# Sequence 1's loads and broadcasts in another order, its layer norm statistics on ScalarE, two scalings on GpSimd

## The chip, the cores and the metric

The kernel runs on one core of a Trainium2 chip. The metric is the device time of one execution in microseconds (us). The engines are called PE (TensorE), DVE (VectorE), ACT (ScalarE), POOL (GpSimd) and SP (SyncE, which here only issues DMA transfers).

## What is computed

A residual x of 2 sequences by 512 tokens by 512 channels goes through four layers, each between two layer norms: `x = x + layernorm(layer(layernorm(x)))`. The layers are a Mamba block, a gated feed-forward layer with 4-bit weights, a small attention inside each token, and a feed-forward layer with an expert. The change lies in the first layer norm and in the Mamba block:

```python
def _layernorm(x, axis=-1, eps=1e-05):
    m = jnp.mean(x, axis=axis, keepdims=True)
    v = jnp.var(x, axis=axis, keepdims=True)
    return (x - m) / jnp.sqrt(v + eps)

def _L0_attn_ref(hidden_states, W_in, conv_w, conv_b, W_x, W_dt, b_dt, A_log, D, W_out):
    D_IN, N, K, R = 1024, 16, 4, 32
    proj = hidden_states @ W_in.T
    x, gate = (proj[..., :D_IN], proj[..., D_IN:])
    xpad = jnp.pad(x, ((0, 0), (K - 1, 0), (0, 0)))
    xc = conv_b
    for j in range(K):
        xc = xc + conv_w[:, j] * xpad[:, j:j + L, :]
    x = silu(xc)
    ssm = x @ W_x.T
    ts, Bm, Cm = (ssm[..., :R], ssm[..., R:R + N], ssm[..., R + N:])
    ts, Bm, Cm = rms_forward(ts), rms_forward(Bm), rms_forward(Cm)
    dt = softplus(ts @ W_dt.T + b_dt)
    A = -jnp.exp(A_log)
    def step(state, inp):
        dt_t, B_t, C_t, u_t = inp
        dA = jnp.exp(dt_t[..., None] * A)
        state = state * dA + (dt_t * u_t)[..., None] * B_t[:, None, :]
        y = jnp.einsum('bdn,bn->bd', state, C_t)
        return (state, y)
    ...
    y = ys + x * D
    y = y * silu(gate)
    return y @ W_out.T
```

`rms_forward` divides by the root of the mean square over the last axis.

## The kernel before

The residual lies in SBUF as eight tiles of 128 tokens by 512 channels, four for each sequence: x0 to x3 for sequence 0, x4 to x7 for sequence 1. Inside the Mamba block the work is turned: 128 channels lie on the partitions and the 512 tokens of a sequence along the free axis, so the 1024 inner channels make eight groups c.

**The head** runs from the start to about 65 us. It normalises sequence 0, projects it into the eight groups (weights `w_x0_*`), convolves, multiplies by W_x into the "ranks" (the 32 rows of dt and the 16 of B and of C) and normalises those in `ranks_norm(0)`. The gate weights `w_g0_0` to `w_g0_2` (L111, in `w4`) are loaded on SP, and the first gate group and half of the second, `half_gate` (L652), are multiplied. `ranks_rows` transposes the normalised ranks (L536); `ranks_out` (L539) copies the dt rows with ScalarE (L541) and the B and C rows, "bc", with VectorE (L542), and writes bc to a DRAM tile, scr. From there `states` (L547) reads it back 16 times on SP (L554), each time two states' rows broadcast over all 128 partitions, 512 KB: the tiles B_0 to B_7 and C_0 to C_7. Behind the last of these broadcasts on SP stand the four x tiles of sequence 1 (`load_x`, L83), and behind those the packed words of the second layer's weights.

**The scan** is a list of 16 items k, one for each pair of sequence and channel group, each in eight steps of two states: 128 steps s. The loop over s writes an order out by hand:

```python
order = [(b, c) for b in range(B) for c in range(NCH)]
```

For each step ScalarE takes two exponentials of 128x511 into one of two PSUM buffers, da (L1039); VectorE multiplies du by the B tile into bx (L1055) and runs the recurrence over 128x1024 in one instruction (TENSOR_TENSOR_SCAN, L1059); GpSimd multiplies bx by the C tile (L1065); and PE adds the two halves into the output, py, with an identity as weights (L1087). The exponentials of step s+2 go into the buffer that scan s has read. There are six bx buffers. For each item ScalarE copies dt into PSUM (L1047) and VectorE multiplies it by u (du, L1053); `fin` multiplies the finished item into its gate (L1093), and dt of the next item comes from a small matmul (L562) and ScalarE's softplus (L567), which changes the activation table. "bx_k_g" below is step g of item k of sequence 0.

**Beside the scan** PE works through one long list, the generator `stream()`: the gates of sequence 0 (L741), the transposes of the normalised sequence 1 (L821), its projections, its ranks (`ranks1`) and their transposed rows (`rows1`), the gates of sequence 1, the output projection, and the second layer for sequence 0. What follows a matmul on the other engines is a small job, spawned with a lag counted in half steps of the scan. A gate's job is three rows of ScalarE (th, g, th: L714, L715, L716) and a product on GpSimd (L719). `norm_job` is such a job: it takes the statistics of x4 to x7 with VectorE's BATCH_NORM instructions, L798 and L799, then ve (L125, variance plus epsilon) on VectorE and, on GpSimd, the power -1/2 (L127) and the product of mean and that, times -1 (L136, L137). `ranks_norm` is run for sequence 1 as a job too; of it the two scalings of the mean squares are L513 and L514 ("rr"), on VectorE. `words_job` unpacks the 4-bit weights between the scan's steps.

Before the scan's loop a call of `pin()` makes each engine keep the order in which the program was written, so an instruction waits for all that stand ahead of it on its engine. SP's transfers are spread over eight completion lanes in turn; from the ninth broadcast on, each issue follows the landing of an earlier one.

Of the kernel before, what the change touches and what calls it, by code (L numbers as in the profile page):

```python
# [9 lines left out]
F32 = mybir.dt.float32  # L10
# [3 lines left out]
ALU = mybir.AluOpType  # L14
# [42 lines left out]
def tile_sandwich(  # L57
# [48 lines left out]
    wgt = const.tile([P, KH, NE], F32, name="wgt")  # L106


    def w4(src, name, chunks=KH, cols=PW):
        t_ = wst.tile([P, KH, PW], F32, tag="w4", name=name)  # L110
        nc.sync.dma_start(out=t_[:, :chunks, :cols], in_=src)  # L111
        return t_

    def moments(srcs, name):
# [311 lines left out]
    with ExitStack() as mamba:  # L426
# [21 lines left out]
        def mbank(name):  # L448
            return ps_m.tile([P, S], F32, tag="m", name=name)
# [18 lines left out]
        def w_in(part, b, c):  # L468

            key = "w", part, b, c // 2  # L470
            if key not in st:
                st[key] = w4(W_in[part * NCH // 2 + c // 2], f"w_{'xg'[part]}{b}_{c // 2}")
            return st[key]
# [28 lines left out]
        def ranks_norm(b, ps):  # L502
# [7 lines left out]
            )  # L510
            nc.vector.tensor_reduce(ss[:, :, 1:], sq[:, :, R_DT // N_ST :], AX.X, ALU.add)
            r = stat.tile([P, TB, 3], F32, tag="rr", name=f"rr{b}")
            nc.vector.tensor_scalar(r[:, :, 0], ss[:, :, 0], 1.0 / R_DT, 1e-6, ALU.mult, ALU.add)  # L513
            nc.vector.tensor_scalar(r[:, :, 1:], ss[:, :, 1:], 1.0 / N_ST, 1e-6, ALU.mult, ALU.add)  # L514
            yield 1
            if b:
                nc.gpsimd.tensor_tensor(r, r, mhalf3, ALU.pow)
# [21 lines left out]
        def ranks_out(b, pt):  # L539
            bc = st["bc"] = jrow(f"bc{b}")  # L540
            nc.scalar.copy(dtT[b][:R_DT, :], pt[:R_DT])  # L541
            nc.vector.tensor_copy(bc[R_B:N_ROW], pt[R_B:N_ROW])  # L542
            sc = dram.tile([N_ROW - R_B, S], F32, tag=f"scr{b}", name=f"scr{b}")
            nc.sync.dma_start(out=sc, in_=bc[R_B:N_ROW])
            scr.append(sc)
# [27 lines left out]
        with ExitStack() as p1:  # L573
# [73 lines left out]
            root = stat.tile([P, 1], F32, tag="root", name="root", bufs=1)  # L647
            nc.scalar.activation(root, half[:, 0:1], AF.Sqrt)

            half_gate = mbank("pg0_1")  # L650
            for k in range(KH // 2):
                nc.tensor.matmul(  # L652
                    half_gate, w_in(1, 0, 0)[:, k, P : 2 * P], xT[0][:, k, :], start=(k == 0), stop=False
                )
            for _ in ranks_norm(0, pr):
                pass
            ranks_out(0, ranks_rows(0, bank1(0, "pt0")))

            for gi in range(NGI):
                if gi + 1 < NGI:  # L660
                    states(0, gi + 1, "B")
                states(0, gi, "C")
            last = states(0, 0, "B")
            gw.word()
            dt_out(0, 0, dt_in(0, 0, bank1(0, "pv0_0")))
            with tc.issue_after(last.ins):
                load_x(1)
            pin()

        g1p = pool(mamba, "mg1", 1)  # L670
# [4 lines left out]
        with ExitStack() as p2:  # L675
# [75 lines left out]
            def gate(b, c):  # L751
                w = w_in(1, b, c)
                if c + 2 - c % 2 < NCH:
                    w_in(1, b, c + 2 - c % 2)
                if (b, c) == (0, 1):
                    turns.append([f"pg{b}_{c}", None])
                    ps = half_gate
                    yield from in_proj(b, ps, w, c % 2, KH // 2)
                else:
                    ps = yield from bank(f"pg{b}_{c}")  # L760
                    yield from in_proj(b, ps, w, c % 2)
                spawn(gate_job(b, c, ps), 2)
# [30 lines left out]
            def norm_job(b, name):  # L793

                mv = stat.tile([P, TB, 2], F32, tag="mv", name=f"mv_{name}")
                for i, src in enumerate(xs(b)):
                    s6 = stat.tile([P, 6], F32, tag="st", name=f"st_{name}_{i}")
                    nc.vector.bn_stats(s6, src)  # L798
                    nc.vector.bn_aggr(mv[:, i, :], s6)  # L799
                    yield 1  # L800
                yield 1
                rs = rstd(mv, name)
                nm = minus_mean(mv, rs, name, TB, True)
                yield 3
                for i in range(TB):
                    yield 2
# [293 lines left out]

            pe = stream()
            spawn(words_job(), 4)
            spawn(norm_job(1, "n1"), 12)

            d0 = jrow("d0")
            nc.vector.tensor_mul(d0, u[0][0], st["dt", 0, 0])
# [373 lines left out]
```

## Time and profile before

| what | us |
|---|---|
| time, median of 3 runs | 957.5 (957.22 to 958.73) |
| the profiled execution's own time | 955.66 |
| its span (first to last instruction) | 953.7 |
| busy: PE | 860.8 |
| busy: VectorE | 672.4 |
| busy: GpSimd | 486.8 |
| busy: ScalarE | 424.1 |
| TensorE clock granted, mean share of full | 0.965 |
| the 128 scans of VectorE (L1059), busy | 291.4 |
| the 127 products with B (L1055), busy | 152.8 |

"Busy" sums the time in which an engine executes; waiting is not in it. The scan stage runs from about 65 to 600 us; behind it come the rest of the second layer and the third and fourth layers, in which PE does most of the work. In rows of the profile `out<-in` names the program's buffers, and the part in square brackets says how long the engine stood before the instruction and what released it. In the chain of waits each row gives start, duration and what the program's end was traced back through.

### The profile page before, as it was taken

To read this page: it belongs to the slowest core of one execution; us is meant where nothing else is said; L and a number is where in the kernel's file an instruction comes from. 1 tells how busy PE (TensorE), PEld (TensorE's weight loads), DVE (VectorE), ACT (ScalarE), POOL (GpSimd) and SP (SyncE) were. 2 spreads that over 40 slices of the span, in tenths; PEclk is the share of its full clock that TensorE was granted. 3 is DMA by queue.
4 is the path that set the end of the run, shared out by engine and by line. 5 is a ranking of instruction groups with operands and counts; after the bars stand their busy time and mean duration, and the time that the engine had idled before them with its cause. 6 is when DMAs were issued, how large, how long until landed. Compare 5 with 4: busy or idle time off the path is not lost.

```text
span 953.7 us, 7163 instructions
## 1 busy us (share of the span) xinstructions
PE 860.8 (90%) x2188; PEld 385.4 (40%) x2188; DVE 672.4 (71%) x780; ACT 424.1 (44%) x638; POOL 486.8 (51%) x356
## 2 busy tenths in 40 slices
PE   6989778789999889589999999999999998999994
PEld 3433333334533434134434444444544444455441
DVE  5877999999999998999999995535600024525225
ACT  4356675656666655476655640125320013412122
POOL 7746796677877787876877884440000000011002
PEclk9989999888999999889999999999999999999998
DMA  6449111010002854200111103445222231100101
GB/s 201 156 141 376 52 37 38 30 37 30 22 23 91 293 194 142 89 0 0 45 44 45 30 9 125 153 156 198 57 65 74 60 101 44 67 12 23 56 0 44
DMA packets 43816, 80.08 MB, mean 84 GB/s; under 512 B 7774, under 2 KB 20937, under 8 KB 43778
## 3 DMA queue, kind: packets, MB, share of 16 engines
q1 hardware_dynamic: 41506, 73.64, 23.4%
q0 software_dynamic: 1984, 5.47, 1.6%
q10 hardware_dynamic: 288, 0.52, 0.1%
q8 instruction: 17, 0.28, 0.1%
q14 instruction: 21, 0.17, 0.1%
HBM read 68.37 MB, written 11.24 MB: 83 GB/s over the span
## 4 chain that ended last, share of the span: by engine, by line
PE 48%; DVE 24%; issue 9%; POOL 7%; DMA 3%; ACT 2%; SPq 0%; DVEq 0%; POOLq 0%; ACTq 0%
DVE bx L1059 10%; DVE bx L1055 6%; PE py L1087 6%; PE pd L1408 6%; POOL bx L1065 5%; PE pup L1345 5%; PE fo L1198 4%; PE fg L371 4%; PE fu L371 4%; PE fo L1261 3%; PE fu L984 3%; PE fg L984 3%; PE po L1176 3%; PE po L953 2%; DVE u L483 2%
## 5 line engine op out<-in xcount | busy, mean ns | idle before, releaser
L1065 POOL TENSOR_TENSOR bx<-bx,C 128x1024 f32<-128x1024 f32 x128 | 301.8, 2358 | 117.4 <-DVE bx L1059 94.2
L1059 DVE TENSOR_TENSOR_SCAN bx<-da,bx 128x1024 f32<-128x1024 f32 x128 | 291.4, 2277 | 0.1
L1087 PE MATMUL py<-bx,ident 128*128 128x512 f32 x480 | 234.9, 620 | 41.4 <-POOL bx L1065 36.3
L1039 ACT ACTIVATE da<-dt,A 128x511 f32<-128x511 f32 x256 | 176.6, 691 | 170.1 <-DVE bx L1059 163.4
L1087 PEld LDWEIGHTS py<-bx,ident 128*128 128x128 f32 x480 | 90.8, 197 | 168.1 <-issue 91.7
L1055 DVE TENSOR_TENSOR bx<-du,B 128x1024 f32<-128x1024 f32 x127 | 152.8, 1203 | 5.7 <-DMA B<-scr 2.2
L1274 DVE TENSOR_TENSOR it<-it,fu 128x512 f32<-128x512 f32 (+1 forms) x11 | 7.5, 686 | 75.2 <-PE fu L371 75.2
L385 POOL TENSOR_TENSOR sd<-ve,half 128x4 f16<-128x4 f16 x2 | 2.1, 1042 | 110.7 <-DVE ve L383 110.7
L1345 PE MATMUL pup<-hT_l,wup 128*128 128x512 f32 x128 | 57.8, 606 | 0.0
L741 PE MATMUL pg<-xT,w_g 128*128 128x512 f32 x116 | 56.5, 619 | 0.0
L1408 PE MATMUL pd<-wdn,hid 128*128 128x512 f32 x128 | 55.3, 593 | 0.0
L127 POOL TENSOR_TENSOR rs_lo<-ve_lo,mhalf 128x1 f32<-128x1 f32 x8 | 5.4, 680 | 76.7 <-DVE ve_lo L125 76.7
L371 PE MATMUL fg<-hT_f,wg 128*128 128x512 f32 (+1 forms) x88 | 41.9, 614 | 0.7 <-ACT hT_f L171 0.7
L984 PE MATMUL fg<-hT_f,wg 128*128 128x512 f32 (+1 forms) x88 | 42.1, 597 | 0.0
L984 PE MATMUL fu<-hT_f,wu 128*128 128x512 f32 (+1 forms) x88 | 40.7, 592 | 0.0
L483 DVE SCALAR_TENSOR_TENSOR u<-px,ch,u 128x511 f32<-128x511 f32 (+2 forms) x48 | 35.8, 746 | 6.9 <-ACT u L476 5.8
L1261 PE MATMUL fo<-wd,it 128*128 128x512 f32 (+1 forms) x88 | 40.5, 603 | 0.0
L371 PE MATMUL fu<-hT_f,wu 128*128 128x512 f32 (+1 forms) x88 | 39.8, 593 | 0.0
L1198 PE MATMUL fo<-wd,it 128*128 128x512 f32 (+1 forms) x88 | 38.0, 594 | 1.8 <-DMA wd<-wd_d 1.8
L1408 PEld LDWEIGHTS pd<-wdn,hid 128*128 128x128 f32 x128 | 24.2, 190 | 30.7 <-issue 30.1
L1345 PEld LDWEIGHTS pup<-hT_l,wup 128*128 128x128 f32 x128 | 24.3, 193 | 28.8 <-issue 28.8
L1273 ACT ACTIVATE it<-fg 128x512 f32<-128x512 f32 (+1 forms) x11 | 6.6, 597 | 65.7 <-PE fg L371 65.7
(238 smaller groups left out, 1164.8 us busy)
## 6 DMA issues: line engine op xcount, KB each, us to landing
wo<-in_W_outT SPq DMA_DIRECT2D x20, 512.0 KB
B<-scr SPq DMA_DIRECT2D x16, 512.0 KB
C<-scr SPq DMA_DIRECT2D x16, 512.0 KB
wg<-wgu_d SPq DMA_DIRECT2D x10, 512.0 KB
wu<-wgu_d SPq DMA_DIRECT2D x10, 512.0 KB
w_x<-in_W_in SPq DMA_DIRECT2D x8, 512.0 KB
wgu_d<-w_gu POOLq DMA_DIRECT2D x16, 256.0 KB, 2.4
w_g<-in_W_in SPq DMA_DIRECT2D x8, 512.0 KB
```

The costliest lines, as they stand in the source:

```text
L371: nc.tensor.matmul(ps[:m], w[:, kc, e * P : e * P + m], hT[:, kc, :], start=(kc == 0), stop=(kc == KH - 1),)
L741: nc.tensor.matmul(ps, w[:, k, ts(e, P)], xT[b][:, k, :], start=(k == 0), stop=(k == KH - 1))
L984: nc.tensor.matmul(ps[:m], wt[j][a][:, kc, e * P : e * P + m], hT[:, kc, :], start=(kc == 0), stop=(kc == KH - 1),)
L1039: nc.scalar.activation(das[s % 2][:, i, 1:], st["dt", b, c][:, 1:], AF.Exp, scale=A[:, c, n : n + 1])
L1055: nc.vector.tensor_mul(bx, st["du"].unsqueeze(1).to_broadcast([P, NG, S]), Bbs[b][gi])
L1059: nc.vector.tensor_tensor_scan(flat, das[s % 2].rearrange("p n t -> p (n t)"), flat, 0.0, ALU.mult, ALU.add)
L1065: nc.gpsimd.tensor_mul(bxs[s], bxs[s], Cbs[b][s % NGI])
L1087: nc.tensor.matmul(st["y"], ident, bx[:, i, :], start=False, stop=last)
L1198: nc.tensor.matmul(fo[t], its[i][:m, ts(t, P)], w[:m, e], start=(i == 0), stop=(i == len(IC) - 1),)
L1261: nc.tensor.matmul(fo[t], its[i][:m, ts(t, P)], w[:m], start=(i == 0), stop=(i == len(IC) - 1),)
L1345: nc.tensor.matmul(ps, w[:, kc, ts(e, P)], src[kc], start=(kc == 0), stop=(kc == KH - 1))
L1408: nc.tensor.matmul(pd, hid[kc][:, ts(i, P)], wdn[kc], start=(kc == 0), stop=(kc == INT // P - 1),)
```

## The change

- **Loads and broadcasts.** `w4` keeps the instructions that it issues in a list. The x tiles of sequence 1 no longer follow the last broadcast; they go on SP right behind the newest gate weights issued at that point, `w_g0_0`, ahead of `w_g0_1`, `w_g0_2` and the write of scr. The broadcasts of sequence 0 were issued as B1 C0 B2 C1 B3 C2 B4 C3 B5 C4 B6 C5 B7 C6 C7 B0; they are issued as B1 B2 C0 B3 C1 B4 C2 B5 C3 B6 C4 B7 C5 C6 C7 B0.
- **The gate in the head.** Three of the four matmuls of the second gate are done in the head, ahead of `ranks_norm(0)`, and one is left for the stream, where it was two and two.
- **Ranks of sequence 1.** The two scalings of the mean squares go from VectorE to GpSimd, and the bc copy from VectorE to ScalarE, behind the dt copy.
- **Statistics of sequence 1.** In `norm_job` the BATCH_NORM instructions are replaced by two passes of ScalarE for each tile: Identity with scale -1/512 and a running sum into `mv`, which gives minus the mean; then Square with that as bias and a running sum, which gives 512 times the variance. Their full outputs go to a scratch tile. ve (now with the scale 1/512), the power and the product are GpSimd's; the factor -1 goes. The job starts with a lag of 2 instead of 12.

The order written for each engine changes with it. On ScalarE the passes stand between exponentials: after those of step 1 and of step 2 the two of x4, after steps 3 and 4 those of x5, around step 6 those of x6, around step 8 those of x7. The applications of the norm (L150) and the transposes of the four tiles come about one step later, as do the convolutions of the channel groups 3 to 6 of sequence 1; the first nibble of one of the unpacked words comes a step earlier. Counted in rows of the instruction order, in which a run of equal instructions is one row, VectorE goes from 763 to 751, ScalarE from 508 to 517, PE from 626 to 628, GpSimd from 360 to 362, and SP stays at 214; the number of activation table loads in the order is 39 in both.

```diff
--- before.py
+++ after.py
@@ -106,9 +106,11 @@
     wgt = const.tile([P, KH, NE], F32, name="wgt")
 
 
+    issued = []
+
     def w4(src, name, chunks=KH, cols=PW):
         t_ = wst.tile([P, KH, PW], F32, tag="w4", name=name)
-        nc.sync.dma_start(out=t_[:, :chunks, :cols], in_=src)
+        issued.append(nc.sync.dma_start(out=t_[:, :chunks, :cols], in_=src))
         return t_
 
     def moments(srcs, name):
@@ -510,8 +512,9 @@
             )
             nc.vector.tensor_reduce(ss[:, :, 1:], sq[:, :, R_DT // N_ST :], AX.X, ALU.add)
             r = stat.tile([P, TB, 3], F32, tag="rr", name=f"rr{b}")
-            nc.vector.tensor_scalar(r[:, :, 0], ss[:, :, 0], 1.0 / R_DT, 1e-6, ALU.mult, ALU.add)
-            nc.vector.tensor_scalar(r[:, :, 1:], ss[:, :, 1:], 1.0 / N_ST, 1e-6, ALU.mult, ALU.add)
+            eng = nc.gpsimd if b else nc.vector
+            eng.tensor_scalar(r[:, :, 0], ss[:, :, 0], 1.0 / R_DT, 1e-6, ALU.mult, ALU.add)
+            eng.tensor_scalar(r[:, :, 1:], ss[:, :, 1:], 1.0 / N_ST, 1e-6, ALU.mult, ALU.add)
             yield 1
             if b:
                 nc.gpsimd.tensor_tensor(r, r, mhalf3, ALU.pow)
@@ -539,7 +542,10 @@
         def ranks_out(b, pt):
             bc = st["bc"] = jrow(f"bc{b}")
             nc.scalar.copy(dtT[b][:R_DT, :], pt[:R_DT])
-            nc.vector.tensor_copy(bc[R_B:N_ROW], pt[R_B:N_ROW])
+            if b:
+                nc.scalar.copy(bc[R_B:N_ROW], pt[R_B:N_ROW])
+            else:
+                nc.vector.tensor_copy(bc[R_B:N_ROW], pt[R_B:N_ROW])
             sc = dram.tile([N_ROW - R_B, S], F32, tag=f"scr{b}", name=f"scr{b}")
             nc.sync.dma_start(out=sc, in_=bc[R_B:N_ROW])
             scr.append(sc)
@@ -647,11 +653,13 @@
             root = stat.tile([P, 1], F32, tag="root", name="root", bufs=1)
             nc.scalar.activation(root, half[:, 0:1], AF.Sqrt)
 
-            half_gate = mbank("pg0_1")
-            for k in range(KH // 2):
+            first_gate = mbank("pg0_1")
+            for k in range(KH - 1):
                 nc.tensor.matmul(
-                    half_gate, w_in(1, 0, 0)[:, k, P : 2 * P], xT[0][:, k, :], start=(k == 0), stop=False
+                    first_gate, w_in(1, 0, 0)[:, k, P : 2 * P], xT[0][:, k, :], start=(k == 0), stop=False
                 )
+            with tc.issue_after(issued[-1].ins):
+                load_x(1)
             for _ in ranks_norm(0, pr):
                 pass
             ranks_out(0, ranks_rows(0, bank1(0, "pt0")))
@@ -659,12 +667,12 @@
             for gi in range(NGI):
                 if gi + 1 < NGI:
                     states(0, gi + 1, "B")
-                states(0, gi, "C")
+                if gi:
+                    states(0, gi - 1, "C")
+            states(0, NGI - 1, "C")
             last = states(0, 0, "B")
             gw.word()
             dt_out(0, 0, dt_in(0, 0, bank1(0, "pv0_0")))
-            with tc.issue_after(last.ins):
-                load_x(1)
             pin()
 
         g1p = pool(mamba, "mg1", 1)
@@ -754,8 +762,8 @@
                     w_in(1, b, c + 2 - c % 2)
                 if (b, c) == (0, 1):
                     turns.append([f"pg{b}_{c}", None])
-                    ps = half_gate
-                    yield from in_proj(b, ps, w, c % 2, KH // 2)
+                    ps = first_gate
+                    yield from in_proj(b, ps, w, c % 2, KH - 1)
                 else:
                     ps = yield from bank(f"pg{b}_{c}")
                     yield from in_proj(b, ps, w, c % 2)
@@ -794,13 +802,23 @@
 
                 mv = stat.tile([P, TB, 2], F32, tag="mv", name=f"mv_{name}")
                 for i, src in enumerate(xs(b)):
-                    s6 = stat.tile([P, 6], F32, tag="st", name=f"st_{name}_{i}")
-                    nc.vector.bn_stats(s6, src)
-                    nc.vector.bn_aggr(mv[:, i, :], s6)
-                    yield 1
-                yield 1
-                rs = rstd(mv, name)
-                nm = minus_mean(mv, rs, name, TB, True)
+
+                    xn = jrow(f"xj_{name}_{i}")
+                    nc.scalar.activation(
+                        xn, src, AF.Identity, scale=-1.0 / H, accum_out=mv[:, i, 0:1]
+                    )
+                    yield 2
+                    nc.scalar.activation(
+                        xn, src, AF.Square, bias=mv[:, i, 0:1], accum_out=mv[:, i, 1:2]
+                    )
+                    yield 2
+                yield from pool_turn()
+                ve = stat.tile([P, TB], F32, tag="ve", name=f"ve_{name}")
+                nc.gpsimd.tensor_scalar(ve, mv[:, :, 1], 1.0 / H, 1e-5, ALU.mult, ALU.add)
+                rs = stat.tile([P, TB], F32, tag="rs", name=f"rs_{name}")
+                nc.gpsimd.tensor_tensor(rs, ve, mhalf, ALU.pow)
+                nm = stat.tile([P, TB], F32, tag="nm", name=f"nm_{name}")
+                nc.gpsimd.tensor_mul(nm, mv[:, :, 0], rs)
                 yield 3
                 for i in range(TB):
                     yield 2
@@ -1100,7 +1118,7 @@
 
             pe = stream()
             spawn(words_job(), 4)
-            spawn(norm_job(1, "n1"), 12)
+            spawn(norm_job(1, "n1"), 2)
 
             d0 = jrow("d0")
             nc.vector.tensor_mul(d0, u[0][0], st["dt", 0, 0])
```

## The prediction

> **What bounds the kernel now.** I read the page's busy shares, the windows of the scan stage, the chain of waits through the stage's first steps, and then VectorE's, GpSimd's and ScalarE's timelines there. The page names a different engine than the windows do:
>
> ```profile
> PE 860.8 (90%) x2188; PEld 385.4 (40%) x2188; DVE 672.4 (71%) x780; ACT 424.1 (44%) x638; POOL 486.8 (51%) x356
> 200.00:300.00 100.00, 90.45 (x244) 41.54 (x245) 96.41 (x72) 63.06 (x97) 75.66 (x41) 0.93 0.07 22
> L1039 ACT ACTIVATE da<-dt,A 128x511 f32<-128x511 f32 x256 | 176.6, 691 | 170.1 <-DVE bx L1059 163.4
> ```
>
> TensorE (PE) leads over the span, but within the scan (the window's columns are the times, then PE, PEld, DVE, ACT, POOL, clock, DMA) VectorE is busy 96% and PE 90%: VectorE sets the pace with PE close behind. ScalarE's exponentials waited 163.4 us for scans: room there, on the average. The change touches two places of VectorE's queue. First the scan's first steps, in the chain and in the timelines:
>
> ```profile
> 69.56 12.32 DMA B<-scr
> 81.90 9.60 DMA x<-in_x_in
> 91.53 0.70 DVE st_n L798
> 92.25 0.18 DVE mv_n L799
> 92.44 2.17 DVE bx L1059
> ...
> 73.60 1.22 DVE L1055 TENSOR_TENSOR bx<-du,B 128x1024 f32<-128x1024 f32 x1 [2.17 <-DMA B<-scr]
> 91.53 0.69 DVE L798 BATCH_NORM_STATS2 st_n<-x 128x6 f32<-128x512 f32 x1 [3.45 <-DMA x<-in_x_in]
> 90.28 0.60 ACT L714 ACTIVATE th<-pg 128x512 f32<-128x512 f32 x1 [1.87 <-PE pg L741]
> 104.53 1.22 DVE L1055 TENSOR_TENSOR bx<-du,B 128x1024 f32<-128x1024 f32 x1
> ```
>
> VectorE stands 3.45 us before the first statistics of sequence 1, because the x tiles queue behind 16 broadcasts of 512 KB; scan and product stand behind that instruction. A product is 1.22 us and a scan 2.28; back to back, a start follows a product by 1.15 and a scan by 2.17 (the last chain row), 3.3 a step. Second, in the middle:
>
> ```profile
> 269.00 1.14 DVE L513 TENSOR_SCALAR rr<-ss 128x4 f32<-128x4 f32 x1
> 270.05 0.16 DVE L514 TENSOR_SCALAR rr<-ss 128x8 f32<-128x8 f32 x1
> 267.75 2.35 POOL L1065 TENSOR_TENSOR bx<-bx,C 128x1024 f32<-128x1024 f32 x1 [1.79 <-DVE bx L1059]
> 286.89 0.68 DVE L542 COPY bc<-pt 32x512 f32<-32x512 f32 x1 [2.84 <-ACT dtT L541]
> 287.61 2.29 DVE L1059 TENSOR_TENSOR_SCAN bx<-da,bx 128x1024 f32<-128x1024 f32 x1
> 291.50 0.60 ACT L714 ACTIVATE th<-pg 128x512 f32<-128x512 f32 x1 [0.15 <-PE pg L741]
> 294.59 0.57 ACT L1047 COPY du<-dt 128x512 f32<-128x512 f32 x1
> ```
>
> The first scaling takes 1.14 us and ends with GpSimd's product (270.10); the same line took 0.16 in the head. The bc copy makes VectorE stand 2.84 us, with the scan behind it.
>
> **Loads and broadcasts, the first steps.** VectorE's gains, on its own queue:
> - The x loads go ahead of w_g_1, so the 3.45 wait goes.
> - The statistics leave VectorE. The four starts, from 91.53 on, cost 0.91, 0.73, 0.82 and 0.80 (one row is 0.69 + 0.18): 3.26. With them goes ve, 0.14, of which 0.05 was not hidden by another wait.
> - B_2 takes the second slot of the queue instead of the third. The ninth and later issues each follow a landing (72.29 for the second slot, 73.60 for the third), so bx_0_2 starts at 72.29, not 73.60: 1.31. C_0 then lands at 73.6 and GpSimd begins 1.2 us later than at 72.44. It had waited 5.37 for C_0, and has 0.9 us of slack in every step (2.36 of 3.3); the walk has it level by bx_0_6. No cost.
>
> Sum 8.07. Walked on VectorE's queue alone, by 1.15 after a product and 2.17 after a scan: bx_0_2 at 72.3, scan 2 at 76.8, bx_0_4 at 78.9, scan 4 at 83.4, bx_0_7 at 89.0, scan 6 at 90.1, du_1 at 92.3, bx_1_0 at 93.1, bx_1_1 at 96.45, against 104.53: 8.1, the sum again. B_3 (fourth slot, landing at 75.5 by the issue that follows it) is 0.1 ahead of its product at 75.6; every later B gains on its product (B_4 78.1 for 78.9, B_7 85.8 for 89.0, B_0 90.9 for 93.1).
>
> What takes part of it back is ScalarE. I walked its queue: exps(2) end at 73.0; the two passes per x tile fit behind, and exps(3) end at 79.7 where scan 3 can start at 80.06, exps(4) at 83.0 where scan 4 needs 83.37, and from there the slack grows (2.8 us at scan 6). Then comes th of gate 4. It waited for PE before (row 90.28) and does again: PE has no gap from 75.3 to 94.3, and the gate's chain starts with dt_1, 0.27 later than now since table load and activation come after tile 0's two passes. So th at 90.5, three rows 1.49, exps(7) to 93.45, and only then the copy of du_1, 0.59, to 94.04. VectorE wanted du_1 at 92.3 and gets it at 94.05, where the row of before is 100.35: 6.3 kept of 8.07. By bx_1_4 it is 6.6, ve's 0.14 and a shorter stand at a copy included. If each pass carries a readout of its accumulator of 0.2 us (not in the trace; a small GpSimd row is 0.20–0.25), 5.9. I take 6.5.
>
> **The statistics on ScalarE.** Eight passes 128x512, SBUF to SBUF. Nearest rows: L716 (immediates) 0.63; L773 with one pointer operand 0.72. So 4 x 0.63 + 4 x 0.72 = 5.4 us of ScalarE for 3.3 of VectorE. The Trainium skill speaks against it: "ScalarE: Activation LUTs", section "Rules for kernel authors", sends adds and multiplies to VectorE and not to ScalarE; its section "What ACT_TABLE_LOAD costs" prices a pass at 186 ns + 0.833 ns an element, 93 ns for a pointer: 0.61 and 0.71, agreeing with the rows. By the rule, with both engines bound, the sum for the statistics is +2.1 us. The trace decides otherwise: ScalarE waited 13 us for scans between 64 and 110, so the passes lie in waits and cost what the du_1 copy shows above. The same section puts a switch of table set at 2.66 us; the trace has the load at 1.28 with the next activation 0.01 behind it. No load is added: the instruction order has 39 before and after.
>
> **Other moves of the head.** The x loads on SP: four issues of 0.3–0.5 us at about 31, and 1 MB beside w_g_0, at some 400 GB/s (the broadcasts' rate) 2.6 us. They push w_g_1, w_g_2 and the scr write back only in order: w_g_0 was issued at 30.83 and PE's row with its first matmul starts at 53.06; SP issues nothing from the last of the gate weights (51.15) to scr (63.29), where w_g_1 (40.46) and w_g_2 find room. The words' loads behind the broadcasts (87.08) come 4 issues earlier. Bounds: 0 to +0.6, taken 0. The third matmul of first_gate sits before the rank transposes: PE's row of four records at 58.14 ends at 60.07, the transposes begin at 61.30 waiting for nb, so two more records of 0.43 fit (60.9): 0, at half clock +0.5. Later PE runs one gate matmul fewer, -0.86. The normalised tiles and their transposes come a step later, so px1_0 waits about 1.3 for the last xT, with a matmul less ahead: 0. GpSimd gets ve and loses the times -1 (0.25): 0; the power (1.04) stays.
>
> **Middle.** Scalings off VectorE: the gap between scan and next product, 268.99 to 270.12, 1.1 us. GpSimd runs two small operations, 0.2–0.25 each, ahead of a product, inside its slack; its power follows anyway. The bc copy with its wait: the scan at 287.61 could start at 284.07, 3.55. But PE had 0.4 us of gaps between 285.65 and 305; th (291.50) is PE's, the du copy (294.59) stands behind it on ScalarE, and the next du product behind that, so this scan's gain lasts until there. Of the 3.55, 1.4 is kept. The copy on ScalarE, 0.57, lies before a th that waits. Bounds of the middle 1.1 and 4.65; taken 2.5, nearer to what PE lets through than to the whole.
>
> **After it.** The orders are written down for each engine, so later stages shift as a whole; PE-filled stretches (433–484, 504–556) begin from points that VectorE or GpSimd release. Sum 6.5 + 2.5 = 9.0. The profiled execution is 955.66 (span 953.7), 1.84 under the median 957.5; the subtraction is made in the profiled run (946.7) and carried to the median: 948.5.
>
> **Rivals.**
> 1. Full gain: th is not waited for, du is ready, PE follows: 8.07 + 4.65 + 0.2 = 12.9, 944.6. Against it: PE without gaps at both places. For it: PE's matmul count ahead falls by one.
> 2. PE is the bound beyond my walk: VectorE's advance returns as waits for PE's gates and sums (PE is 90% busy against 96%), half the head and little of the middle left, about 4: 953.5. For it: windows with PE at 97.86% between 500 and 600, and a granted clock of 0.50 between 64.5 and 71.3 which may move.
> 3. Slower: the passes hold the exponentials. Place: exps(3) and exps(4), with slack of 0.3–0.4 us. The gain of 9 and some 2.5 of slack are gone when each of the eight costs about 1.4 us more on the scans' path, for instance a table load before and another after each: 8 x 2.56 = 20.5, less 11.5: +9, 966.5. Against it: the rows 0.63 and 0.72, and 39 loads in both orders. At +0.4 a pass only some 2 us are lost.
> 4. The loads do not come early, held behind w_g_1's buffer wait: the passes on ScalarE then hold the exponentials of a whole step, 0 to +2: about 957.5. SP's order speaks against it.
>
> **How the numbers follow.** Forecast (gain 6.5 to 11) 0.54, full gain 0.12, PE bound 0.20, slower 0.10, no effect 0.04. Range: full gain with 1 us of run-to-run (957.2 to 958.7) 943.5; low end, rival 2 with 1 us, 954.5; outside it the slower case and half of the fourth. Own range of the likeliest: 946.5–951. A measurement of this kernel tells 0.2% (1.9 us) from none. Faster 0.86, same 0.04, slower 0.10.
>
> **What the next profile shows.** Right: no wait for x in VectorE's timeline; bx_0_2 near 72.3, bx_1_1 near 98.2; du_1 there waits up to 2 us for ScalarE, which waits for PE's gate; passes of 0.6–0.75 each; the scan after the rank rows near 284 less 6.5, then a wait for du. Wrong: scans 3 or 4 wait for exps, passes of 1 us or more, 43 or more table loads, VectorE's scan share unchanged with PE's idle smaller, or the gain at 105 us not kept at 600.

## The result, and the profile after

| | before | changed |
|---|---|---|
| median, us | 958.24 (957.22 to 960.64, 6 runs) | 950.05 (946.45 to 951.93, 6 runs) |
| ratio, 95% interval | | 0.9906 (0.9883 to 0.993) |
| profiled execution: span, us | 953.7 | 944.5 |

The change makes the kernel 8.2 us faster by the medians; the interval of the ratio is 6.7 to 11.2 us. The forecast was 9.0. A second comparison of the same kernel gave 949.98 against 957.61, ratio 0.9927 (0.9904 to 0.995). Its profile has a span of 948.1, and the two profiles of one program, side by side, say most about this change. The first is of the fastest of its six executions (946.45), the second of a middle one (950.21). In the table stand the starts of VectorE's scans (their instruction is L1077 now), and in brackets how much earlier they are than before. The scans count from 0, eight to an item: scan 8 is the first of item 1.

| start of scan | before | changed, first profile | changed, second profile |
|---|---|---|---|
| 0 (end of the head) | 68.04 | 68.01 (0.03) | 67.50 (0.54) |
| 8 | 105.67 | 99.55 (6.12) | 101.77 (3.90) |
| 12 | 120.85 | 113.89 (6.96) | 116.12 (4.73) |
| 47 (ahead of the scalings) | 265.30 | 258.23 (7.07) | 260.45 (4.85) |
| 56 (behind the bc copy) | 301.67 | 292.02 (9.65) | 294.26 (7.41) |
| 127 (the last) | 569.83 | 559.80 (10.03) | 561.84 (7.99) |

The middle gives 2.6 us in both profiles (9.65 - 7.07, 7.41 - 4.85). The first steps give 6.1 in one and 3.9 in the other. Between scan 56 and the last another 0.4 and 0.6 are added.

The shares of busy time and of the chain of waits, from the changed kernel's page:

```profile
PE 859.0 (91%) x2188; PEld 384.5 (41%) x2188; DVE 666.7 (71%) x768; ACT 429.2 (45%) x655; POOL 487.0 (52%) x358
PE 52%; DVE 25%; issue 8%; POOL 5%; ACT 4%; DMA 1%; DVEq 0%; POOLq 0%; SPq 0%; ACTq 0%
```

DMA fell from 3% of the chain to 1% and PE rose from 48% to 52%. The same program part in VectorE's timeline, first profile (start, duration, then what it waited for):

```profile
75.22 1.22 DVE L1073 TENSOR_TENSOR bx<-du,B 128x1024 f32<-128x1024 f32 x1 [0.48 <-DMA B<-scr]
80.00 2.29 DVE L1077 TENSOR_TENSOR_SCAN bx<-da,bx 128x1024 f32<-128x1024 f32 x1 [0.24 <-ACT da L1057]
94.20 0.70 DVE L1071 TENSOR_TENSOR du<-u,du 128x512 f32<-128x512 f32 x1 [1.85 <-ACT du L1065]
98.44 1.20 DVE L1073 TENSOR_TENSOR bx<-du,B 128x1024 f32<-128x1024 f32 x1
```

The 3.45 us wait for x is gone; 0.48 is waited for a B tile, bx_0_3's. Scan 3 stands 0.24 for its exponentials, the place of the third rival, and in this profile no more. The only long wait is at du_1, and the last row is bx_1_1, at 104.53 before. ScalarE's timeline tells who holds du_1:

```profile
69.61 0.62 ACT L807 ACTIVATE xj_n<-x 128x512 f32<-128x512 f32 x1
70.13 0.19 ACT L807 ACTIVATION_READ_ACCUMULATOR xj_n<-x 128x1 f32 x1
73.04 0.71 ACT L811 ACTIVATE xj_n<-x,mv_n 128x512 f32<-128x512 f32 x1
73.65 0.19 ACT L811 ACTIVATION_READ_ACCUMULATOR xj_n<-x,mv_n 128x1 f32 x1
73.85 1.28 ACT L573 ACT_TABLE_LOAD   x1
90.75 0.60 ACT L722 ACTIVATE th<-pg 128x512 f32<-128x512 f32 x1 [2.34 <-PE pg L749]
93.60 0.57 ACT L1065 COPY du<-dt 128x512 f32<-128x512 f32 x1
```

The passes (L807, L811) take 0.62 and 0.71 and are each followed by a row that reads the sum. th of gate 4 waits 2.34 for PE's gate, and the du_1 copy comes when its three rows and a pair of exponentials are through.

In the middle, from the timelines of GpSimd, VectorE and ScalarE:

```profile
263.12 0.20 POOL L516 TENSOR_SCALAR rr<-ss 128x4 f32<-128x4 f32 x1
268.61 0.69 DVE L1111 TENSOR_TENSOR g<-g,py 128x512 f32<-128x512 f32 x1 [1.09 <-PE py L1105]
276.97 2.28 DVE L1077 TENSOR_TENSOR_SCAN bx<-da,bx 128x1024 f32<-128x1024 f32 x1
278.67 0.58 ACT L546 COPY bc<-pt 32x512 f32<-32x512 f32 x1
286.74 0.69 DVE L1071 TENSOR_TENSOR du<-u,du 128x512 f32<-128x512 f32 x1 [0.86 <-ACT du L1065]
```

A scaling is 0.20 us on GpSimd. Scan 52 (276.97) no longer stands behind the bc copy; ahead of it fin waits 1.09 for PE, and behind it du ("du_7" below, for item 7) waits 0.86 for ScalarE. These two waits are new. In the second profile fin doesn't wait and du_7 waits 2.07.

### The profile page after: what moved, and what is told of

It is laid out like the page before. It is cut to its first block, busy times and chain, and to the rows that moved or that the text cites. A ratio compares the mean times of both kernels' runs of the same rounds, so it can differ in the third digit from the quotient of the medians.

```text
span 944.5 us, 7179 instructions
## 1 busy us (share of the span) xinstructions
PE 859.0 (91%) x2188; PEld 384.5 (41%) x2188; DVE 666.7 (71%) x768; ACT 429.2 (45%) x655; POOL 487.0 (52%) x358
## 4 chain that ended last, share of the span: by engine, by line
PE 52%; DVE 25%; issue 8%; POOL 5%; ACT 4%; DMA 1%; DVEq 0%; POOLq 0%; SPq 0%; ACTq 0%
DVE bx L1077 9%; PE py L1105 8%; DVE bx L1073 7%; PE pd L1426 6%; PE pup L1363 5%; PE fo L1216 4%; PE fu L373 3%; PE fo L1279 3%; PE fg L373 3%; PE fu L1002 3%; PE po L1194 3%; PE fg L1002 3%; POOL bx L1083 3%; PE po L971 2%; DVE u L485 2%
## 5 line engine op out<-in xcount | busy, mean ns | idle before, releaser
L1077 DVE TENSOR_TENSOR_SCAN bx<-da,bx 128x1024 f32<-128x1024 f32 x128 | 292.1, 2283 | 0.3 <-ACT da L1057 0.2
```

Of the source, the lines that this page charges most:

```text
L1077: nc.vector.tensor_tensor_scan(flat, das[s % 2].rearrange("p n t -> p (n t)"), flat, 0.0, ALU.mult, ALU.add)
```

## The experiments

Where a number of us is given for a scan, it is from the profile, against the kernel named. The medians scatter: over 14 profiles the time from the start of the last scan to the end of the span, where nothing was edited, lies between 382.1 and 388.1 us. So small differences are read from the scans' starts.

**The loads alone** (on the kernel before):

```diff
+            with tc.issue_after(issued[-1].ins):
+                load_x(1)
             for _ in ranks_norm(0, pr):
...
-            with tc.issue_after(last.ins):
-                load_x(1)
```

> The kernel before with one part of the change alone: sequence 1's x tiles are loaded behind w_g0_0. Theory (VectorE's queue sets the pace until ScalarE's copy of du_1 can bind): the 3.45 us wait before the first statistics goes and nothing replaces it, since du_1 would be wanted at 100.35 - 3.45 = 96.9, later than the 94.0 at which ScalarE can have it. Scan 8 starts at 105.67 - 3.45 = 102.2, and the gain stays 3.4 us to the last scan. Rival 1 (PE is the bound): less than 2 us left at scan 8, with waits for PE's gate or for py in place. Rival 2 (the loads disturb the head): scan 0, at 68.04 before, starts 0.5 us or more later.

Median 952.3 (951.16 to 956.52, 7 runs) against 957.03, ratio 0.9949 (0.9925 to 0.9973). Scan 8 at 101.86, 3.81 earlier; the last scan 4.46 earlier. Its VectorE timeline:

```profile
87.72 0.68 DVE L801 BATCH_NORM_STATS2 st_n<-x 128x6 f32<-128x512 f32 x1
88.54 2.26 DVE L1062 TENSOR_TENSOR_SCAN bx<-da,bx 128x1024 f32<-128x1024 f32 x1
```

The statistics start with no wait in brackets, and the scan follows: the wait for x was worth its full length, and moving four loads early cost the head nothing (scan 0 at 67.92).

**All but the statistics** (on the changed kernel):

```diff
-                    nc.scalar.activation(xn, src, AF.Identity, scale=-1.0 / H, accum_out=mv[:, i, 0:1])
...
+                    nc.vector.bn_stats(s6, src)
+                    nc.vector.bn_aggr(mv[:, i, :], s6)
...
-            spawn(norm_job(1, "n1"), 2)
+            spawn(norm_job(1, "n1"), 12)
```

> The changed kernel with the statistics of sequence 1 back on VectorE (BATCH_NORM instructions, lag 12). Theory: of the 3.3 us that the statistics cost VectorE only part is lost, because in the changed kernel VectorE stands 1.85 us at du_1 for ScalarE: scan 8 at 99.55 + 3.3 - 1.85 = 101.0, and the kernel about 1.4 us slower than the changed one to the end. Rival 1 (the statistics are worth all they cost): scan 8 at 102.8, 3.3 us slower. Rival 2 (the passes on ScalarE cost as much as they save): the same as the changed kernel or faster.

Median 948.46 (947.34 to 949.06, 4 runs), ratio 0.9907 (0.9875 to 0.9939). Scan 8 at 100.90, as the theory had it, and the last scan 3.04 behind the changed kernel's first profile, where 1.4 was expected. But the time is not longer than the changed kernel's. So both were run again on one chip:

> The changed kernel once more, to be compared on one chip with the three others of this call, and to see another profile of it. Theory (half-clock windows of PE move the head): if PE waits for dt_1 under 1 us at about 75, the twelve gate rows behind it take 5.4 us and scan 8 starts near 99.5; if it reached that wait early and stood 2 us or more, they take over 7 us and scan 8 starts 1.5 to 2.7 us later. Rival (the spread of the other profiles comes from their edits): scan 8 within 0.3 of 99.55 again, counted from scan 0 at 68.01. Time 948 to 951.5.

> The changed kernel with the statistics on VectorE again, in more rounds than the first time. Theory 1 (the passes on ScalarE give back what VectorE saves, through dt_1 and PE's half clock): within 1.5 us of the changed kernel in the same call. Theory 2 (the profile of the changed kernel is typical): 2 to 3 us slower than it.

The changed kernel: 949.98 (947.9 to 953.65, 6 runs), ratio 0.9927 (0.9904 to 0.995). With the statistics on VectorE: 947.24 (946.99 to 947.97, 4 runs), ratio 0.9895 (0.9876 to 0.9914). Over both comparisons the medians are 949.99 (12 runs) and 947.70 (8 runs). The statistics on ScalarE bring no gain in the time. The medians point to a loss of 2.3 us; the two intervals still overlap a little, so the loss itself isn't settled. The scans don't show a loss: the last one starts at 559.80 and 561.84 in the changed kernel's two profiles, and at 562.84 and 561.69 with the statistics on VectorE. Behind it, where both are the same program, the changed kernel takes 384.7 and 386.3, the other 384.1 and 383.8, all within the scatter given above. So what takes the gain back is only in part to be seen at the first steps. That part is in PE's rows. The changed kernel's first profile, PE's timeline, and the windows (in these the third number from the end is the granted clock):

```profile
66.58 7.42 PE L749 MATMUL pg<-xT,w_g 128*128 128x512 f32 x10
75.80 5.42 PE L749 MATMUL pg<-xT,w_g 128*128 128x512 f32 x12 [0.74 <-ACT dt L573]
...
66.00:72.00 6.00, 6.00 (x8) 2.33 (x8) 5.22 (x5) 5.92 (x12) 1.28 (x2) 0.50 0.86 244
74.00:81.00 7.00, 6.26 (x15) 2.61 (x15) 6.27 (x5) 6.93 (x12) 7.00 (x4) 1.00 1.03 417
```

And its second profile:

```profile
65.74 4.56 PE L749 MATMUL pg<-xT,w_g 128*128 128x512 f32 x10
75.45 7.98 PE L749 MATMUL pg<-xT,w_g 128*128 128x512 f32 x12 [3.35 <-ACT dt L573]
...
66.00:72.00 6.00, 5.32 (x12) 1.85 (x11) 5.69 (x6) 5.92 (x12) 0.94 (x2) 1.00 0.97 274
74.00:81.00 7.00, 5.55 (x7) 2.38 (x8) 6.12 (x5) 6.18 (x10) 7.00 (x5) 0.53 1.02 415
```

In the first profile PE ran its ten gate rows at half clock, came late to gate 3 and stood 0.74 us there for dt_1; then the twelve rows ran at full clock, in 5.42. In the second the ten rows ran at full clock in 4.56; PE came early, stood 3.35 us, and the granted clock then fell to half for the next rows: 7.98. Two waits of VectorE follow from it, in the second profile:

```profile
81.81 0.60 ACT L722 ACTIVATE th<-pg 128x512 f32<-128x512 f32 x1 [1.55 <-PE pg L749]
84.75 2.29 DVE L1077 TENSOR_TENSOR_SCAN bx<-da,bx 128x1024 f32<-128x1024 f32 x1 [1.70 <-ACT da L1057]
96.42 0.70 DVE L1071 TENSOR_TENSOR du<-u,du 128x512 f32<-128x512 f32 x1 [2.75 <-ACT du L1065]
```

th of gate 3 waits 1.55 for PE's rows, and the exponentials that stand behind it on ScalarE come late for scan 4, which waits 1.70 (in the first profile it doesn't wait). At du_1, behind th of gate 4, VectorE waits 2.75 where it was 1.85. From scan 0 to scan 8 the second profile takes 34.27 us and the first 31.54; 1.7 of the difference lies at scan 4 and 0.9 at du_1. As scan 0 was 0.5 earlier, 2.2 is left of it at scan 8. Of the seven profiles of kernels with the early passes and three gate matmuls in the head, two show the short stand (0.74 and 0.78), five a stand of 2.00 to 4.10 with twelve rows of 7.1 to 8.0 us behind it. Both profiles with the statistics on VectorE show 0.69 and 5.42:

```profile
75.70 5.42 PE L749 MATMUL pg<-xT,w_g 128*128 128x512 f32 x12 [0.69 <-ACT dt L573]
```

But in both of these PE's ten rows ahead ran mostly at half clock (7.26 and 6.47 us), as in the changed kernel's first profile, and gate 3 then starts at about the same time with the passes (75.80) and without (75.93, 75.70). How the kernel with the statistics on VectorE fares when PE comes early was not seen, and whether the passes make that case more frequent isn't shown.

**The broadcasts in the order of before** (on the changed kernel):

```diff
-                if gi:
-                    states(0, gi - 1, "C")
-            states(0, NGI - 1, "C")
+                states(0, gi, "C")
```

> The changed kernel with sequence 0's broadcasts in the order of before (C0 ahead of B2). No engine's order changes. Theory (ScalarE's du_1 copy behind PE's gate sets scan 7): scan 2 starts 1.3 us later, VectorE's wait at du_1 shrinks from 1.85 to about 0.5, and at scan 8 0 to 0.3 us are lost. Rival (VectorE's queue sets scan 7): 1.3 us later at scan 8 and to the end.

Median 949.3 (947.7 to 951.11, 4 runs), ratio 0.9921 (0.9899 to 0.9943). Scan 2 starts 1.80 later than in the changed kernel's first profile (1.3 was expected), scan 8 0.12 earlier; PE stood 0.78 in this profile, so the two can be compared. VectorE's timeline:

```profile
73.70 1.22 DVE L1071 TENSOR_TENSOR bx<-du,B 128x1024 f32<-128x1024 f32 x1 [2.36 <-DMA B<-scr]
94.08 0.70 DVE L1069 TENSOR_TENSOR du<-u,du 128x512 f32<-128x512 f32 x1 [0.39 <-ACT du L1063]
```

The wait for the broadcast (2.36) comes back, the wait at du_1 shrinks to 0.39, and du_1 starts when it did. The new order is worth nothing as long as ScalarE's copy ends this stretch.

**Each pass twice** (on the changed kernel; the same for Square):

```diff
+                    nc.scalar.activation(xn, src, AF.Identity, scale=-1.0 / H)
                     nc.scalar.activation(
                         xn, src, AF.Identity, scale=-1.0 / H, accum_out=mv[:, i, 0:1]
```

> The changed kernel with each of the eight statistics passes run once more without its sum (8 extra rows of 0.52 to 0.61 us on ScalarE, the same scratch tile). Theory: exps(3) and exps(4) are late by 1.1 and 1.6 us and scans 3 and 4 wait for them; the later slack gives part back, gate 4's th and the du_1 copy come about 1.0 later, so scan 8 is 1.0 us later and 0.5 to 1 is left at scan 12. Rival (every pass lies on the scans' path): the whole 4.5 us at scan 8. Rival 2 (ScalarE has room for all): nothing lost at scan 8.

Median 948.18 (945.66 to 953.55, 4 runs), ratio 0.9912 (0.9878 to 0.9946): no loss in the time. Its VectorE timeline:

```profile
80.48 2.29 DVE L1079 TENSOR_TENSOR_SCAN bx<-da,bx 128x1024 f32<-128x1024 f32 x1 [2.26 <-ACT da L1059]
84.95 2.29 DVE L1079 TENSOR_TENSOR_SCAN bx<-da,bx 128x1024 f32<-128x1024 f32 x1 [1.07 <-ACT da L1059]
96.62 0.70 DVE L1073 TENSOR_TENSOR du<-u,du 128x512 f32<-128x512 f32 x1 [2.75 <-ACT du L1067]
```

Scans 3 and 4 wait for exponentials, as expected, though the part of half-clocked gates in this isn't separated (scan 4 of the second profile waits 1.70 without the extra passes). PE stood 4.10 here, so the second profile of the changed kernel is the one to compare with: scan 8 at 101.97 against 101.77. Its scan 0 was 0.59 earlier, so the price at scan 8 is 0.2 to 0.8 us for 5.6 us of added work (an extra Identity pass puts off the next row by 0.65, an extra Square by 0.74). The third rival needed some 1.4 us more for each pass on the scans' path; it is out.

**The middle alone** (on the kernel before: the two scalings on GpSimd, the bc copy on ScalarE, as in the diff of the change):

> The kernel before with only the two moves at the ranks of sequence 1: the scalings on GpSimd, the bc copy on ScalarE. Theory: PE has no gaps there, so the scan behind the scalings starts 1.1 us earlier and the one behind the copy 4.7 us earlier, but by scan 56 only 2.5 us are left (2.6 in the changed kernel). Rival (both gains are VectorE's and stay): 4.7 us at scan 56 and after. Second rival (GpSimd's two operations delay its products): nothing left at scan 50.

Median 953.55 (951.0 to 959.39, 20 runs) against 957.03, ratio 0.9966 (0.9954 to 0.9979). VectorE's timeline:

```profile
270.60 2.28 DVE L1065 TENSOR_TENSOR_SCAN bx<-da,bx 128x1024 f32<-128x1024 f32 x1
277.40 0.69 DVE L1099 TENSOR_TENSOR g<-g,py 128x512 f32<-128x512 f32 x1 [1.21 <-PE py L1093]
285.77 2.28 DVE L1065 TENSOR_TENSOR_SCAN bx<-da,bx 128x1024 f32<-128x1024 f32 x1
295.47 0.70 DVE L1059 TENSOR_TENSOR du<-u,du 128x512 f32<-128x512 f32 x1 [0.81 <-ACT du L1053]
```

Against before, and counted from scan 47: 1.12 earlier at scan 48 (270.60), 0.19 later at scan 50 (fin's 1.21), 3.44 earlier at scan 52 (285.77) and 2.51 at scan 56. At scan 69 another 1.4 us is lost in this profile, in a wait of 2.93 for a bx buffer where the changed kernel's first profile waits 1.47. The profiled execution was the slowest of the 20 (959.39), so the median stands on its own here.

**One move of the middle taken back** (on the changed kernel):

```diff
-            eng = nc.gpsimd if b else nc.vector
+            eng = nc.vector
```

> The changed kernel with the two scalings of sequence 1's mean squares back on VectorE. Theory (PE is the bound there): scan 48 starts 1.1 us later against its neighbours, and at scan 50 nothing of it is left, because fin of item 5 in the changed kernel waits 1.09 us for PE's py anyway; from scan 52 on 0 to 0.3 us later, the time as the changed kernel's. Rival (the forecast's split, 1.1 of 2.5): 1.1 us later from scan 48 to the end.

```diff
-            if b:
-                nc.scalar.copy(bc[R_B:N_ROW], pt[R_B:N_ROW])
-            else:
-                nc.vector.tensor_copy(bc[R_B:N_ROW], pt[R_B:N_ROW])
+            nc.vector.tensor_copy(bc[R_B:N_ROW], pt[R_B:N_ROW])
```

> The changed kernel with the bc copy of sequence 1 back on VectorE. Theory: VectorE stands for PE's transposes and ScalarE's dt copy (at 278.65 in the changed kernel), so scan 52 starts 2.4 us later; at scan 55 the 0.86 us wait for du vanishes, and 1.6 us are left to the end. Rival 1 (the copy carries the whole gain of the middle): 2.5 us left at scan 56. Rival 2 (VectorE's wait was hidden by PE): under 0.5 us left.

Medians 951.54 (ratio 0.9935, 0.9911 to 0.996) and 952.74 (0.9946, 0.9927 to 0.9965). Both profiles had the long stand in the head, so they are compared with the changed kernel's second profile, from scan 47 on. (In that one fin doesn't wait for PE ahead of scan 50: the scans come later there than in the first and PE is level with them.) Scalings on VectorE: 1.12 later at scan 48, still 1.12 at scan 52 and 1.10 at scan 56. bc on VectorE: 3.63 later at scan 52, where 2.4 was expected, and 1.43 at scan 56 (1.6 was expected). My theory for the scalings (0 to 0.3 left) missed, since it took the 1.09 of the first profile for a fixed wait; the forecast's 1.1 was right. By the last scan the two kernels are 2.24 and 2.33 behind; the rest comes at scan 69, in a wait for a bx buffer (2.42 and 2.17, in the changed kernel's second profile 1.25), and why it is longer stays open. PE's timeline of the kernel with the scalings on VectorE:

```profile
276.43 1.98 PE L1105 MATMUL py<-bx,ident 128*128 128x512 f32 x4 [1.18 <-POOL bx L1083]
279.46 1.98 PE L1105 MATMUL py<-bx,ident 128*128 128x512 f32 x4 [1.04 <-POOL bx L1083]
```

The later scans make GpSimd's products later, and PE waits for them twice, where the changed kernel's second profile has one such wait, of 1.05. From there on PE has no gap, and the added 1.18 reaches VectorE at du_7, through th and the copy on ScalarE. In the kernel with bc on VectorE, the wait at the copy is back at its old length, and du_7 no longer waits:

```profile
280.61 0.68 DVE L545 COPY bc<-pt 32x512 f32<-32x512 f32 x1 [2.83 <-ACT dtT L544]
290.16 0.67 DVE L1068 TENSOR_TENSOR du<-u,du 128x512 f32<-128x512 f32 x1
```

**Gate 4's rows behind the du_1 copy** (on the changed kernel):

```diff
                 release(f"pg{b}_{c}")
+                if (b, c) == (0, 4):
+                    yield 2
                 yield from silu_of(gc, ps, trow(f"th{b}_{c}"))
```

> The changed kernel with the three ScalarE rows of gate 4 two half steps later, so that exps(7), the copy of du_1 and a statistics pass stand ahead of them; no other order of PE or VectorE changes. Theory (the du_1 copy is held by th, th by PE's gate): VectorE's 1.85 us wait at du_1 goes, scan 8 starts at 97.7 instead of 99.55. PE ran without a gap until 105.6, so of the 1.85 us between 0.5 and 1.85 are left by scan 12. Rival (PE sets the end of this stretch): scan 8 earlier, but fin of item 0 waits for py and nothing is left by scan 12. Rival 2 (the copy was held by something else): no change at du_1.

Median 950.29 (944.52 to 953.69, 11 runs), ratio 0.9911 (0.9884 to 0.9938). VectorE's timeline:

```profile
93.51 0.67 DVE L1073 TENSOR_TENSOR du<-u,du 128x512 f32<-128x512 f32 x1
105.71 0.69 DVE L1113 TENSOR_TENSOR g<-g,py 128x512 f32<-128x512 f32 x1 [0.72 <-PE py L1107]
```

The wait at du_1 is gone: scan 7 follows scan 6 by 4.21 us, not 6.17. This profile had PE standing 2.44 with half clock behind it, so scan 6 was already 1.24 late and scan 8 came at 98.83, not 97.7. From scan 6 to scan 12 it takes 23.01 us, the changed kernel's first profile 23.82: 0.8 of the 2.0 us is left, behind fin's wait for PE. At scan 19 this profile loses it again:

```profile
137.23 7.54 PE L749 MATMUL px<-xT,w_x 128*128 128x512 f32 x12 [0.68 <-ACT xT L844]
143.90 2.32 DVE L485 SCALAR_TENSOR_TENSOR u<-px,ch,u 128x511 f32<-128x511 f32 x3 [2.17 <-ACT u L478]
```

The granted clock was 0.50 from 135 to 140 us, the first projection of sequence 1 came late, and VectorE waited 2.17 for it; in the changed kernel's first profile these twelve rows took 5.42 and VectorE didn't wait. In the median nothing shows.

**The passes behind dt_1, and the same with gate 4's rows behind the du_1 copy** (on the changed kernel; the edit at gate 4 is the one above):

```diff
                         xn, src, AF.Identity, scale=-1.0 / H, accum_out=mv[:, i, 0:1]
                     )
-                    yield 2
+                    yield 1
...
-            spawn(norm_job(1, "n1"), 2)
+            spawn(norm_job(1, "n1"), 5)
```

> The changed kernel with the statistics passes started three half steps later and each tile's two closer together, so that dt_1 stands ahead of them all; the transposes come half a step earlier on PE. Theory: dt_1 is ready 0.7 to 1.3 us earlier, PE's wait ahead of gate 3 (0.74 to 4.1 us in the profiles so far) shrinks by as much and its twelve rows run at full clock; th of gate 4 and the du_1 copy come 0.7 us earlier than in the changed kernel's profile, so scan 8 at 98.8, and the median 1 to 2 us under that of the changed kernel. Rival (dt_1 is not what holds PE): no difference at PE's row behind dt_1 and none in the median.

> The same, and gate 4's three rows on ScalarE behind the copy of du_1. Theory: nothing holds VectorE at du_1 any more, scan 7 follows scan 6 by 4.2 us (6.2 in the changed kernel), scan 8 at 97.7, and of the 1.85 us about 1 is left at scan 12, behind PE's py. Median 1.5 to 3 us under the changed kernel's. Rival (PE bounds the stretch to scan 12 in any order): the same as passes_later from scan 12 on.

Medians 949.25 (946.75 to 951.34, 6 runs; ratio 0.9913, 0.9893 to 0.9933) and 947.53 (941.93 to 949.53, 6 runs; 0.9891, 0.9867 to 0.9914). In the first PE reached the clock's long case again, with a stand of 2.61 and twelve rows of 6.91, but the rows started at 74.55, where the changed kernel's two profiles have 75.45 and 75.80. Counted from scan 0 that is 6.61 against 7.95 in the second profile, which has the long case too: dt_1 does hold PE there. Scan 4 doesn't wait, and scan 8 came at 99.79, 2.0 earlier than in that profile. The expected 98.8 was missed, and the gain in the median (0.7) can't be told from none. In the second, VectorE's timeline:

```profile
90.36 2.28 DVE L1079 TENSOR_TENSOR_SCAN bx<-da,bx 128x1024 f32<-128x1024 f32 x1
92.55 0.67 DVE L1073 TENSOR_TENSOR du<-u,du 128x512 f32<-128x512 f32 x1
94.57 2.28 DVE L1079 TENSOR_TENSOR_SCAN bx<-da,bx 128x1024 f32<-128x1024 f32 x1
```

Nothing holds du_1, scan 8 is at 97.88 (97.7 expected), and at the last scan 0.91 us is left against the changed kernel's better profile. Its median is 2.4 us under the changed kernel's of the same comparison (949.98), with intervals that overlap a little, and level with the kernel that leaves the statistics on VectorE (947.24), with far less editing in that one. These two have the lowest medians of all.

## Why the prediction was right

- **The total.** 948.5 was forecast, 950.05 measured; the sign holds, and so does the mechanism of the loads and of the middle. Among the terms one failed, the statistics. That the total came so near all the same is in part luck. By the medians the loads alone gain 4.7 us (interval 2.6 to 7.2) and the middle alone 3.5 (2.0 to 4.4), which is the whole 8.2; the forecast had 3.45 and 2.5 for these two and some 3 for the rest, which shows no gain in the time.
- **The wait for x, 3.45 us.** Right: with the loads alone scan 8 came 3.81 earlier.
- **What ScalarE takes back.** The walk had du_1 at 94.05 and bx_1_1 at 98.2; the first profile has 94.20 and 98.44, so 6.1 of the 8.07 is kept (before, du_1 starts at 100.27 in VectorE's timeline), for the reason given: th behind PE's gate, the copy behind th. The step that the gate's chain starts "0.27 later than now" was mis-sized a little: gate 3's twelve rows started at 75.80 in the first profile, and before at about 75.3 (a row of 14 records at 74.47, of which two, of 0.43 each, belong to gate 2). What the sum left out weighs more: in five other profiles PE stood 2.0 to 4.1 us at this point and ran on at half clock, and in the second profile scan 4 waited 1.70 and du_1 came at 96.42. There 4.73 is left at scan 12, where about 6.6 was forecast. The second rival named the clock as a thing that may move, but the sum took full clock. The stand has two possible causes, the passes ahead of dt_1 and the missing gate matmul: before, a matmul of gate 2 stood between dt_1's own matmul and gate 3, and the row at 74.47 has no wait. Moving the passes away made the stand shorter (2.61 against 3.35) and did not end it; the matmul was not tried alone.
- **The statistics.** The walk credited VectorE with 3.26 for them, of which the cap left some 1.5 (6.3 with all parts, 4.8 for the loads and the broadcasts). That is the part of the sum that failed: 949.99 with them on ScalarE, 947.70 without. The passes themselves cost what was said, 4 x 0.61 + 4 x 0.71 = 5.3 us of ScalarE from start to start against 5.4, and twice as many cost at most 0.8. Where PE comes early, what costs is where the first two stand, ahead of dt_1; what else takes the gain back, behind the scans too, stays open. The rule of the Trainium skill ("ScalarE: Activation LUTs", section "Rules for kernel authors") to leave adds and multiplies to VectorE stood for my sum of +2.1, and the medians lie nearer to that than to a gain. I set it aside because ScalarE waits 13 us in this stretch, and those waits were real, but not ahead of dt_1.
- **The order of the broadcasts, 1.31 us.** Counted in VectorE's sum and taken back by the cap: right, it is worth nothing here (0.12).
- **The middle, 2.5 us.** Right in the sum (2.58, 2.56) and in its parts: 1.1 for the scalings, 1.4 for the copy (1.10 and 1.43 against the second profile), where 1.1 and 1.4 were forecast. That PE had hardly any gaps was the reason, and the waits of 1.09 and 0.86 in the first profile, or of 2.07 in the second, show it.
- **What the changed profile was to show.** No wait for x, passes of 0.6 to 0.75, bx_1_1 at 98.44 (98.2), the scan behind the rank rows at 276.97 (277.5), a wait for du behind the copy: all there. "Scans 3 or 4 wait for exps" was named as a sign against it. In the first profile scan 3 does, by 0.24, without effect; in the second scan 4 does, by 1.70, with effect. The exponentials are late there behind a gate that waits for PE, and not through the price of the passes.
- **The rivals.** Full gain (12.9): no, PE holds both places. Slower through the passes: no, though its place was the right one to watch. The loads do not come early: no. PE beyond my walk: in part, through the clock.

## What to carry to other kernels

When an engine has waits to spare, ask which of its instructions stands behind the added work and who waits for that one: eight passes fit into ScalarE's waits for scans, but the first two stood ahead of the one activation for which PE waits, and when PE came early they put it off. Take the gain of a part on the bound engine only up to the next wait that it will meet, here du_1, and then try the parts alone: of the parts here the early loads and the moves at the ranks carried the gain, and the statistics, the part with most new code, carried none. Where two profiles of one program differ by as much as an edit is worth, read differences between the same two instructions inside a profile, not its end.

## What the runs showed of the hardware that I had not expected

- Ahead of gate 3 a stand of PE of 2.0 to 4.1 us was followed by half clock for the next rows in all six profiles that have one (12 rows in 6.9 to 8.0 us, 5.42 at full clock); stands of 0.69 to 0.78 were not. But the length of a stand does not decide alone. In the kernel before, PE stood 2.62 us ahead of this row and ran on at a granted clock of 1.00:

```profile
97.09 1.98 PE L1087 MATMUL py<-bx,ident 128*128 128x512 f32 x4 [2.62 <-POOL bx L1065]
```

- A stand of 2.22 ahead of one and the same row of the changed kernel was followed by four records in 3.66 us in the first profile (at 321.55) and in 1.98 in the second (at 323.79). The Trainium skill, "TensorE: Matmul & The Clock Gate", section "What's actually happening", describes a clock gate that looks at windows of about 3.4 us that run freely; that fits in that the same program shows both cases and that equal stands end differently. But stands of 2.0 and 2.4 us sufficed, shorter than a window. It calls the penalty of the ramp under 1% of a typical kernel's span; here it is some 2 us at scan 8, 0.2% of the span, which is small and yet as large as the parts under test.
- A sum taken along with an activation is a row of its own, ACTIVATION_READ_ACCUMULATOR, 0.18 to 0.19 us, of which 0.09 adds to the pass: the next row starts 0.61 behind an Identity pass with a sum (69.61 to 70.22), and 0.52 behind the third row of a gate, which is an Identity pass of the same size without one (71.17 to 71.69).
- The first scaling takes 1.14 us on VectorE beside a product on GpSimd, and 0.20 on GpSimd itself.
